# A graph layer on one core: slot numbers from smaller matmuls, edge rows evicted seven and six tiles at a time through two pairs of PSUM banks, loads on another queue

## The chip, the cores and the metric

The kernel runs on one core of a Trainium2 chip. The metric is the device time of one execution in microseconds (us). The kernel before takes 2601.75 us (median of 3 runs, 2600.41 to 2601.91). The profile shows one of these executions, the one of 2600.41 us.

A core has five engines that matter here: TensorE (PE in the profile, with PEld for its weight loads), VectorE (DVE), ScalarE (ACT), GpSimd (POOL) and SyncE (SP). ACT, SP and POOL also issue DMA transfers, each from a queue of its own.

## The reference

The reference is one graph layer with a residual and a layer norm. There are 6250 nodes with 64 features and 206250 directed edges (100000 both ways, and a loop at each node), sorted by destination, each with 64 edge features.

```
row, col = src, dst                       # per edge
msg  = concat(x[col], edge_attr)          # [206250, 128]
h    = relu(msg @ W1a.T + b1a) @ W1b.T + b1b
agg  = segment_sum(h, row) / max(count(row), 1)
z    = relu(concat(x, agg) @ W2a.T + b2a) @ W2b.T + b2b
out  = layernorm(x + concat(z, x) @ Wr.T + br)
```

The second matrix of the edge network is applied after the sum, so an edge contributes a row of 128 hidden values (after the ReLU) to the node `row`. The edges are sorted by `col`, so the rows have to be brought together by `row`.

## The kernel before

**Tiling.** The edges are cut into 1612 tiles of 128, and the tiles into 124 groups of 13. Nodes are numbered in 49 bins of 128. Since edges are sorted by destination, the destinations of one group lie in a window of few nodes: a group's right-hand operand `rhs` holds the 64 edge features of its 1664 edges and, below them, a one-hot row block that picks the node of the window; the weights `mv` hold W1a's edge half and the window's rows of x times W1a.

**The way of an edge row.** For each tile, one fp32 matmul (`hidden`, L949; the profile has two records for each) gives 128 edges by 128 hidden values in PSUM. ACT evicts several tiles at once with the ReLU into `orow` (L950). POOL then scatters the 13 tiles of a group into an array in device memory, one indirect DMA per tile (`scatter`, L956); an edge goes to a slot within the region of the bin of its source node. Later, SP reads the bins back (`read`, L1005), DVE makes a one-hot block from the node numbers (`nodes_of`, L1031 and L1034), TensorE sums the rows by node (`summed`, L1050), and DVE adds the partial sums (`collect`, L1106). Groups of such sums are called sum groups; an epoch is a run of groups that share a slot array (82, 17, 14, 7 and 4 groups).

**Slot numbers.** The slot of an edge is the number of edges with the same bin that come before it in its epoch. For group k, DVE writes a block of 50 bins by 14 columns: the first column of a bin carries the running count (L830), the other 13 say which tile's edge in this partition has this bin (`bins`, L831). A scan (L837) makes running sums from it (`had`). TensorE adds over partitions: with a matrix of ones on `had` (L850) and a matrix of "partition before" and a large diagonal on `bins` (L851), each in two halves of 25 bins, 350 and 325 columns, into two PSUM banks `cnt_ps`. The large diagonal lifts the entry of an edge's own bin above the rest, so one maximum over the bins (L867, in `slots`) picks it, and L872 turns it into the row number `rowidx` that the scatter uses.

**Order of the work.** PE, ACT, DVE and SP run in the order in which the program is written; POOL runs its scatters in order. One iteration k of the main loop does, in this order:

1. `group(k + 3)`: loads for three groups ahead. The edge features (`edges`, L700, 416 KB), the places in the window (L912, 208 KB), a register load (L916) and the window's table rows (L918). From group 8 on ACT issues them, before that SP.
2. ACT's cast of node numbers into `orow` (L1182).
3. TensorE's counting matmuls for group k + 1 (L850, L851).
4. `hidden` of group k in three parts of 4, 3 and 3 tiles.
5. `window(k + 2)` for the first groups, which have no table yet; DVE's `columns(k + 2)`, the one-hot block of `rhs` (L929), and `bins_of(k + 2)`.
6. For k = 6 to 18 a node step (`nodes_ahead`, L1150 to L1160): a matmul for x with W2a, one with Wr, and after DVE's negation a second matmul into the second half of the same PSUM tile.
7. The sum groups that are due, and after the first of them `slots(k + 1)`; after the second (or the first, if only one is due) the last part of `hidden`, 3 tiles, and then the 13 scatters.

After the loop come the remaining sums and the last node step for each three bins (means, transpose, two matrix layers, residual, layer norm, output).

**Buffers around the change.** PSUM: two banks for counting, two buffers for the sums, and the pool `hps` with three separate buffers of one bank each. Parts of `hidden`, windows, the node steps, the table rows (`y_rows`) and the tail all take their PSUM tiles from this pool in turn:

```
            for k0, n in parts:
                ps = hp.tile([P, SUB, H], F32, name="h_ps")
                ...
                nc.scalar.activation(orow[:, k0 : k0 + n, :H], ps[:, :n, :], AF.Relu)
```

SBUF: four `rhs` (EDGES), four `mv`, five `orow` (ROWS), nine read buffers (READS). A sum group is issued to SP when its reads fit in the READS buffers beside those that are still in use.

Of the kernel before, what the change touches and what calls it, by code (L numbers as in the profile page):

```python
# [8 lines left out]
F32 = mybir.dt.float32  # L9
# [8 lines left out]
P = 128  # L18
# [445 lines left out]
ROWS, EDGES, READS = 5, 4, 9  # L464
# [13 lines left out]
def fast_path(  # L478
# [161 lines left out]
    eye_b = const.tile([P, P], F32, name="eye_b")  # L640
    nc.vector.tensor_scalar(eye_b, diff_i, 0.0, BIG, op0=ALU.is_equal, op1=ALU.mult)
# [36 lines left out]
    with (  # L678
# [6 lines left out]
        tc.tile_pool(name="hps", bufs=3, space=PSUM) as hp,  # L685
# [11 lines left out]


        def edges(g):
            (nc.sync if g < NEAR else nc.scalar).dma_start(rhss[g % EDGES][:D, :], edgeT[:, g * NG * P : (g + 1) * NG * P])  # L700
# [25 lines left out]
        def y_rows(b_lo, b_hi):  # L726
            for b0 in range(b_lo, b_hi, SUB):
                n = min(SUB, b_hi - b0)
                ps = hp.tile([P, SUB, H], F32, name="h_ps")
# [26 lines left out]
        nc.vector.scalar_tensor_tensor(  # L756
            before_w, diff_i, 0.0, eye_b, op0=ALU.is_gt, op1=ALU.add
        )
        state = {"rt": 0, "bad": 3}
# [5 lines left out]
        none_b = const.tile([P, 2 * HALF], BF16, name="none_b")  # L765
        nc.vector.memset(none_b, 0.0)
# [52 lines left out]
        hads = {}  # L819

        def bins_of(k):


            ep_ = epoch_of[k]
            c0 = k * BLK
            oh = slp.tile([P, 2 * HALF * T], BF16, name="bins")
            had = slp.tile([P, 2 * HALF * T], BF16, name="had")
            by_bin = oh.rearrange("p (b t) -> p b t", t=T)
            was = none_b if k == ep_.first else state["had"][:, :, BLK]
            nc.vector.tensor_tensor(by_bin[:, :, 0], was, on.rearrange("p (b t) -> p b t", t=T)[:, :, 1], op=ALU.mult)  # L830
            nc.vector.tensor_tensor(  # L831
                by_bin[:, :, 1:],
                ramp[:, : 2 * HALF, None].to_broadcast([P, 2 * HALF, BLK]),
                hi[:, None, c0 : c0 + BLK].to_broadcast([P, 2 * HALF, BLK]),
                op=ALU.is_equal,
            )
            nc.vector.tensor_tensor_scan(had, on, oh, 0.0, op0=ALU.mult, op1=ALU.add)  # L837
            oh, had = (v.rearrange("p (b t) -> p b t", t=T) for v in (oh, had))
            state["had"] = hads[k] = had
            return oh, had  # L840

        def counts_of(oh, had):

            ps = slpp.tile([P, 2, 512], F32, name="cnt_ps")
            for i in range(2):
                v = ps[:, i, : HALF * T].rearrange("p (b t) -> p b t", t=T)
                b = slice(i * HALF, (i + 1) * HALF)
                nc.tensor.matmul(v, one_w, had[:, b, :], start=True, stop=False)  # L850
                nc.tensor.matmul(v[:, :, :BLK], before_w, oh[:, b, 1:], start=False, stop=True)  # L851
            return ps

        def slots(k, ps):
# [4 lines left out]
            if at == 0:  # L859
# [3 lines left out]
                    state["bin"], hi[:, c0 : c0 + m], float(STRIDE), -BIG, op0=ALU.mult, op1=ALU.add  # L863
                )
            v = ps[:, :, : HALF * T].rearrange("p i (b t) -> p i b t", t=T)
            row = slp.tile([P, T], F32, name="row")
            nc.vector.tensor_reduce(row, v.rearrange("p i b t -> p t i b"), axis=mybir.AxisListType.XY, op=ALU.max)  # L867

            def by_now(t):
                nc.vector.tensor_copy(t.rearrange("p (i b) -> p i b", i=2), v[:, :, :, BLK])  # L870

            s = nc.vector.scalar_tensor_tensor(  # L872
                rowidx[:, c0 : c0 + BLK], row[:, :BLK], BIG + STRIDE - 1,
                state["bin"][:, at : at + BLK], op0=ALU.min, op1=ALU.add,
            )
            state["slots"] = s.ins
            if k + 1 == EARLY:
                by_now(early)
                wrong(early, epochs[0].low, ALU.is_gt, slp)
            for st in ep_.steps[:-1]:  # L880
                if k + 1 == st.at:
                    full = slp1.tile([P, 2 * HALF], F32, name="full")
                    by_now(full)
                    wrong(full, st.hi, ALU.is_lt, slp)
            if k + 1 == ep_.end:
                by_now(ep_.tot)
                unused(ep_)

                if (ep_.end - ep_.first) * BLK > 255:
                    most = slp.tile([P, 2 * HALF], F32, name="most")  # L890
                    nc.vector.tensor_scalar(
                        most, hads[k][:, :, BLK], 255.5, None, op0=ALU.is_gt, op1=ALU.add,
                        accum_out=bad[:, state["bad"] :][:, :1],
                    )
                    state["bad"] += 1

        def group(g):
# [14 lines left out]
            s = nc.scalar.dma_start(  # L912
                rel, relt[g : g + 1, :].rearrange("o (h e) -> o h e", h=2).to_broadcast([WIN, 2, half])
            )
            with tc.issue_after(s.ins):
                w = nc.scalar.value_load(win_i[0:1, g : g + 1], min_val=0, max_val=N - WIN)  # L916
            m = mv[g % MV]
            nc.scalar.dma_start(m[D:, :], ytab[bass.ds(w, WIN), :])  # L918
# [15 lines left out]
        def window(g):  # L934

            ps = hp.tile([P, H], F32, name="h_ps")
# [239 lines left out]
        for k, ep_ in enumerate(epoch_of):  # L1176
# [11 lines left out]
            if k + 1 < NGR:  # L1188
                counts = counts_of(*ahead)
# [243 lines left out]
```

## Time and profile before

| | before |
|---|---|
| median of 3 runs | 2601.75 us |
| the profiled execution | 2600.41 us |
| its span, first to last instruction | 2598.5 us |
| mean granted TensorE clock | 0.713 |
| POOL: first scatter starts, last scatter ends | 17.5 us, 2477.7 us |
| POOL: one scatter, 1612 of them | 0.96 us |
| ACT: evictions L950 | 496, mean 0.516 us |
| DVE busy | 1174.2 us |
| bytes moved, mean rate | 375.22 MB, 144 GB/s |

The granted clock is the share of its full speed that TensorE was allowed; in the page's clock row each digit is one fortieth of the span, in tenths. A line of the group list names line, engine, operation, output and inputs, shapes and count; then busy time and the mean of one in ns; then the engine's idle time just before these instructions and what ended most of it. In the list of waits, the numbers are the total in us, how often, and the longest. "remote" is a releaser that the profile could not name. In the timeline the columns are start, duration, engine, line, operation, output and inputs, how many instructions the row joins, and in brackets the idle time before and what ended it.

### The profile page before, as it was taken

The numbers are of one execution on the slowest core, as the hardware profiler recorded it, in microseconds if no ns is written. First come the engines' busy times: TensorE is split into PE (matmuls) and PEld (weight loads), VectorE is DVE, ScalarE is ACT, GpSimd is POOL, SyncE is SP. The second block draws the span as 40 slices with busy tenths as digits, with TensorE's granted clock in tenths as the row PEclk, the third lists the DMA queues.
The fourth block names the chain that finished last, engine by engine and source line by source line (L and its number), as shares of the span: only waits on it lengthen the run. The fifth ranks groups of instructions, "written<-read, shape, count | busy, mean of one in ns | idle before, by whom it ended". The sixth has DMA issues, their size and how long they took to land.

```text
span 2598.5 us, 25106 instructions
## 1 busy us (share of the span) xinstructions
PE 1444.2 (56%) x8253; PEld 1265.4 (49%) x8253; DVE 1174.2 (45%) x1993; ACT 325.1 (13%) x807; POOL 1555.7 (60%) x1630
## 2 busy tenths in 40 slices
PE   3646553444455445454544566565566655666796
PEld 2535443334345344343444555564555555555795
DVE  5233343333334334343433444463545445545587
ACT  1211111111111010110110100110001000110106
POOL 6566666666666666666666665656556666666500
PEclk7656675666766667676766677786777777677898
DMA  6568556444444444343444455544545645555581
GB/s 160 158 207 259 167 164 186 139 115 124 115 121 134 118 117 121 108 133 107 135 125 115 128 157 148 155 136 118 141 143 144 176 139 142 151 151 152 170 261 39
DMA packets 198784, 375.22 MB, mean 144 GB/s; under 512 B 47098, under 2 KB 113980, under 8 KB 198516
## 3 DMA queue, kind: packets, MB, share of 16 engines
q1 hardware_dynamic: 86050, 145.73, 20.1%
q10 hardware_dynamic: 61010, 120.39, 17.2%
q0 software_dynamic: 51584, 107.40, 13.1%
q8 instruction: 67, 1.10, 0.2%
q14 instruction: 73, 0.60, 0.1%
HBM read 221.77 MB, written 151.59 MB: 144 GB/s over the span
## 4 chain that ended last, share of the span: by engine, by line
PE 30%; another core or an unknown queue 28%; issue 18%; DVE 14%; DMA 3%; ACT 3%; ACTq 2%; SPq 0%; DVEq 0%
PE sum_ps L1050 13%; PE h_ps L949 12%; DVE oh L1034 4%; DVE rhs L929 3%; DMA rhs<-relt 2%; DVE had L837 2%; ACT orow L950 2%; PE cnt_ps L851 1%; PE cnt_ps L850 1%; DVE part L1106 1%; DVE row L867 1%; DVE bins L831 1%; PE h_ps L1159 1%; DMA rt<-rows 1%
## 5 line engine op out<-in xcount | busy, mean ns | idle before, releaser
L956 POOL DMA_INDIRECT rows<-orow,rowidx x1612 | 1547.8, 960 | 921.4 <-issue 452.3
L949 PE MATMUL h_ps<-mv,rhs 128*128 128x128 f32 x3224 | 639.8, 349 | 612.7 <-issue 400.2
L949 PEld LDWEIGHTS h_ps<-mv,rhs 128*128 128x128 f32 x3224 | 573.7, 257 | 689.2 <-issue 458.9
L1050 PE MATMUL sum_ps<-rt,oh 128*128 128x129 f32 x4006 | 615.3, 309 | 265.8 <-issue 233.7
L1050 PEld LDWEIGHTS sum_ps<-rt,oh 128*128 128x128 f32 x4006 | 574.1, 223 | 294.1 <-issue 256.8
L950 ACT ACTIVATE orow<-h_ps 128x512 f32<-128x512 f32 x496 | 239.5, 516 | 1814.5 <-remote 1025.1
L1106 DVE TENSOR_TENSOR part<-part,sum_ps 128x258 f32<-128x258 f32 (+2 forms) x183 | 86.4, 473 | 512.0 <-remote 352.8
L929 DVE TENSOR_TENSOR rhs<-rhs,ramp 64x1664 f32<-64x1664 bf16 x116 | 219.4, 1892 | 186.8 <-DMA rhs<-relt 113.2
L867 DVE TENSOR_REDUCE row<-cnt_ps 128x14 f32<-128x700 f32 x124 | 109.3, 882 | 344.7 <-remote 272.2
L837 DVE TENSOR_TENSOR_SCAN had<-ramp,bins 128x700 bf16<-128x700 bf16 x124 | 200.3, 1615 | 4.2
L1034 DVE TENSOR_TENSOR oh<-ramp,node 128x512 f32<-128x512 f32 (+3 forms) x237 | 187.3, 790 | 8.0
L1034 DVE TENSOR_TENSOR oh<-ramp,rt 128x512 f32<-128x512 f32 (+3 forms) x213 | 137.1, 693 | 4.7 <-issue 4.6
L850 PE MATMUL cnt_ps<-had,one_w 128*128 128x350 bf16 x248 | 96.8, 393 | 68.4 <-issue 49.1
L851 PE MATMUL cnt_ps<-bins,before_w 128*128 128x325 bf16 x248 | 97.8, 397 | 39.0 <-issue 38.1
L831 DVE TENSOR_TENSOR bins<-ramp,hi 128x650 bf16<-128x650 f32 x124 | 108.2, 873 | 0.0
L1031 DVE SCALAR_TENSOR_TENSOR node<-unused,rt 128x4 f32<-128x4 bf16 (+3 forms) x237 | 37.4, 158 | 136.5 <-DMA rt<-rows 126.3
L851 PEld LDWEIGHTS <-before_w 128*128 128x128 bf16 x248 | 28.4, 115 | 90.0 <-issue 78.6
L1155 DVE TENSOR_SCALAR zT<-h_ps 128x512 f32<-128x512 f32 (+1 forms) x13 | 8.6, 661 | 123.3 <-PE h_ps L1154 72.4
L1182 ACT CAST orow<-lo 128x13 f32<-128x13 bf16 x124 | 26.6, 214 | 301.8 <-issue 136.8
L1150 PE MATMUL h_ps<-zT,w2x_t 65*128 65x512 f32 (+1 forms) x26 | 21.8, 936 | 73.2 <-ACT orow L950 68.7
L850 PEld LDWEIGHTS <-one_w 128*128 128x128 bf16 x248 | 29.7, 120 | 65.8 <-issue 56.9
L830 DVE TENSOR_TENSOR bins<-had,ramp 128x50 bf16<-128x50 bf16 x119 | 44.1, 371 | 3.6
(113 smaller groups left out, 393.9 us busy)
## 6 DMA issues: line engine op xcount, KB each, us to landing
rt<-rows SPq DMA_DIRECT2D x242, 260.0 KB
rhs<-in_edgeT ACTq DMA_DIRECT2D x116, 416.0 KB
rt<-rows SPq DMA_DIRECT2D x106, 390.0 KB
rows<-orow,rowidx POOLq DMA_INDIRECT x1612
rhs<-relt ACTq DMA_DIRECT2D x116, 208.0 KB
rows<-padrow ACTq DMA_DIRECT2D x4, 4680.0 KB
rows<-padrow ACTq DMA_DIRECT2D x8, 2340.0 KB
rt<-rows SPq DMA_DIRECT2D x48, 325.0 KB
```

The lines of the kernel that those rows point to most:

```text
L831: nc.vector.tensor_tensor(by_bin[:, :, 1:], ramp[:, : 2 * HALF, None].to_broadcast([P, 2 * HALF, BLK]), hi[:, None, c0 : c0 + BLK].to_broa ...
L837: nc.vector.tensor_tensor_scan(had, on, oh, 0.0, op0=ALU.mult, op1=ALU.add)
L850: nc.tensor.matmul(v, one_w, had[:, b, :], start=True, stop=False)
L851: nc.tensor.matmul(v[:, :, :BLK], before_w, oh[:, b, 1:], start=False, stop=True)
L867: nc.vector.tensor_reduce(row, v.rearrange("p i b t -> p t i b"), axis=mybir.AxisListType.XY, op=ALU.max)
L929: nc.vector.tensor_tensor(rhs[D:, :].rearrange("p (h e) -> p h e", h=2), rel, in_win[D:, :, None].to_broadcast([WIN, 2, NG * P // 2]), op= ...
L949: nc.tensor.matmul(ps[:, j, :], rhs[:, c * P : (c + 1) * P], m, start=True, stop=True)
L950: nc.scalar.activation(orow[:, k0 : k0 + n, :H], ps[:, :n, :], AF.Relu)
L956: s = nc.gpsimd.indirect_dma_start(out=ep_.rows, out_offset=bass.IndirectOffsetOnAxis(ap=rowidx[:, t : t + 1], axis=0), in_=orow[:, j, :], ...
L1034: nc.vector.tensor_tensor(res[:, at_tile : at_tile + nb * n, :], ramp[:, None, :].to_broadcast([P, nb * n, P]), node[:, :, None].to_broadc ...
L1050: nc.tensor.matmul(of_bin(b), oh[:, at_tile, :], rt[:, j * n + t, : H + 1], start=t0 + t == st.lo[b], stop=t0 + t == st.hi[b] - 1,)
L1106: nc.vector.tensor_add(to, to, g.ps[:, : g.nb, :])
```

## The change

**Slots.** The scan now starts from zero in every group, so it gives an edge's number within its partition and bin (`nth`). A running total of 50 bins per partition is kept in a small tile `had` (one operation of 50 columns per group). The count of edges before those of this partition, the base, comes from two matmuls of 50 columns into one PSUM tile: ones on the totals of the groups before, and "partition before" on this group's counts. DVE then adds base and number for 13 edges by 50 bins, lifts the entry of an edge's own bin with a multiply-add, and takes the maximum. The totals over all partitions, which some checks at 11 places need, get a matmul of their own there (`counted`). The tiles of the 13 columns are two persistent ones, set to zero once.

**Edge rows.** The pool `hps` has one tile of four banks. `bank(n)` hands out the next n banks of it in turn. A group's `hidden` has two parts, of 7 and 6 tiles, each in two banks and evicted by one ACT operation; the part of 6 comes where the last part of 3 was. Everything else that used the pool takes one bank, and a node step takes three.

**Loads.** SP issues all of a group's loads, in front of the reads of iteration k. There are 8 read buffers instead of 9.

```
-ROWS, EDGES, READS = 5, 4, 9
+ROWS, EDGES, READS = 5, 4, 8
...
-        tc.tile_pool(name="hps", bufs=3, space=PSUM) as hp,
+        tc.tile_pool(name="hps", bufs=1, space=PSUM) as hp,
...
+        banks = hp.tile([P, 4, 512], F32, name="h_ps")
+        state = {"rt": 0, "bad": 3, "bank": 0}
+
+        def bank(n=1):
+            i = -(-state["bank"] // n) * n % 4
+            state["bank"] = (i + n) % 4
+            return banks[:, i : i + n, :].rearrange("p i f -> p (i f)")
...
-            (nc.sync if g < NEAR else nc.scalar).dma_start(rhss[g % EDGES][:D, :], ...)
+            nc.sync.dma_start(rhss[g % EDGES][:D, :], ...)
...
         def bins_of(k):
-            nc.vector.tensor_tensor(by_bin[:, :, 0], was, on..., op=ALU.mult)
             nc.vector.tensor_tensor(
-                by_bin[:, :, 1:],
+                ohs[k % 2][:, :, 1:],
...
-            nc.vector.tensor_tensor_scan(had, on, oh, 0.0, op0=ALU.mult, op1=ALU.add)
+            nc.vector.tensor_tensor_scan(
+                nth, on, ohs[k % 2].rearrange("p b t -> p (b t)"), 0.0, op0=ALU.mult, op1=ALU.add
+            )
...
+                nc.vector.scalar_tensor_tensor(
+                    had, hads[k - 1], 1.0, nths[k][:, :, BLK], op0=ALU.mult, op1=ALU.add
+                )
...
-                nc.tensor.matmul(v, one_w, had[:, b, :], start=True, stop=False)
-                nc.tensor.matmul(v[:, :, :BLK], before_w, oh[:, b, 1:], start=False, stop=True)
+        def bases_of(k):
+            if k > 0:
+                counted(k - 1)
+            first_ = k == epoch_of[k].first
+            if not first_:
+                nc.tensor.matmul(bases, one_w, hads[k - 1], start=True, stop=False)
+            nc.tensor.matmul(bases, before_w, nths[k][:, :, BLK], start=first_, stop=True)
...
-            nc.vector.tensor_reduce(row, v.rearrange("p i b t -> p t i b"), axis=mybir.AxisListType.XY, op=ALU.max)
+            nc.vector.tensor_tensor(
+                own, bases[:, :, None].to_broadcast([P, 2 * HALF, BLK]), nths[k][:, :, 1:], op=ALU.add
+            )
+            nc.vector.scalar_tensor_tensor(own, ohs[k % 2][:, :, 1:], BIG, own, op0=ALU.mult, op1=ALU.add)
+            row = slp.tile([P, BLK], F32, name="row")
+            nc.vector.tensor_reduce(row, own.rearrange("p b t -> p t b"), axis=mybir.AxisListType.X, op=ALU.max)
...
         def group(g):
-            s = nc.scalar.dma_start(
+            s = nc.sync.dma_start(
...
-            nc.scalar.dma_start(m[D:, :], ytab[bass.ds(w, WIN), :])
+            nc.sync.dma_start(m[D:, :], ytab[bass.ds(w, WIN), :])
...
         def hidden(k, parts):
-                ps = hp.tile([P, SUB, H], F32, name="h_ps")
+                ps = bank(2).rearrange("p (j h) -> p j h", h=H)
...
         def nodes_ahead(b0):
-            xp = hp.tile([P, 2, SUB, D], F32, name="h_ps")
+            xp, np_ = (bank().rearrange("p (j d) -> p j d", d=D) for _ in range(2))
...
-                hidden(k, ((0, 4), (4, 3), (7, 3)))
+                hidden(k, ((0, 7),))
...
-                        hidden(k, ((10, 3),))
+                        hidden(k, ((7, 6),))
```

## The prediction

> **What bounds the kernel now.** I read the page first: busy shares, clock row, costliest groups.
>
> ```profile
> PE 1444.2 (56%) x8253; PEld 1265.4 (49%) x8253; DVE 1174.2 (45%) x1993; ACT 325.1 (13%) x807; POOL 1555.7 (60%) x1630
> ...
> PEclk7656675666766667676766677786777777677898
> ...
> L956 POOL DMA_INDIRECT rows<-orow,rowidx x1612 | 1547.8, 960 | 921.4 <-issue 452.3
> L950 ACT ACTIVATE orow<-h_ps 128x512 f32<-128x512 f32 x496 | 239.5, 516 | 1814.5 <-remote 1025.1
> L867 DVE TENSOR_REDUCE row<-cnt_ps 128x14 f32<-128x700 f32 x124 | 109.3, 882 | 344.7 <-remote 272.2
> L837 DVE TENSOR_TENSOR_SCAN had<-ramp,bins 128x700 bf16<-128x700 bf16 x124 | 200.3, 1615 | 4.2
> L831 DVE TENSOR_TENSOR bins<-ramp,hi 128x650 bf16<-128x650 f32 x124 | 108.2, 873 | 0.0
> L830 DVE TENSOR_TENSOR bins<-had,ramp 128x50 bf16<-128x50 bf16 x119 | 44.1, 371 | 3.6
> ```
>
> No engine is full. POOL issues 1612 scatters of 0.96 us with 0.30 us between them: 1.266 us each, 16.46 us per group of 13, 2041 us in all. Its first starts at 17.5 us, its last ends at 2477.7; what remains is a tail of 121 us. Its other idle time is 422 us in 119 stalls, and the list of waits names the cause:
>
> ```profile
> ACT orow L950 <- remote: 1025.1, 104, 24.7
> ACT orow L950 <- PE h_ps L949: 548.9, 85, 17.5
> ...
> POOL rows L956 <- ACT orow L950: 405.1, 120, 14.4
> ...
> PEld h_ps L949 <- ACT orow L950: 220.3, 30, 16.6
> PE h_ps L949 <- ACT orow L950: 208.3, 28, 16.3
> ```
>
> POOL waits for ACT's evictions, ACT for TensorE. Of the stalls, 76 stand before a group's tile 10 (the part that is computed behind the sums) and 36 before tile 0. The timeline of one cycle shows their form:
>
> ```profile
> 1042.18 0.95 POOL L956 DMA_INDIRECT rows<-orow,rowidx  x1 [0.30 <-issue]
> ...
> 1045.75 0.49 ACT L950 ACTIVATE orow<-h_ps 128x384 f32<-128x384 f32 x1 [15.21 <-remote]
> ...
> 1046.52 0.95 POOL L956 DMA_INDIRECT rows<-orow,rowidx  x1 [3.38 <-ACT orow L950]
> ...
> 1048.66 1.35 ACT L950 ACTIVATE orow<-h_ps 128x512 f32<-128x512 f32 x3
> ...
> 1069.73 1.36 ACT L950 ACTIVATE orow<-h_ps 128x512 f32<-128x512 f32 x3 [6.46 <-remote]
> 1070.61 0.96 POOL L956 DMA_INDIRECT rows<-orow,rowidx  x1 [4.21 <-ACT orow L950]
> ```
>
> POOL runs dry at 1043.13; ACT and DVE's L867 get TensorE's results only 2.62 us later, both at 1045.75, and POOL restarts at 1046.52. The second stall is alike: dry at 1066.40, results at 1069.73. Between stalls TensorE runs at its own pace for about 5 us after POOL's restart and then crawls: from about 1079 to 1101 its matmul records come 0.7, 1.4 or 2.1 us apart, and at 1101.66, after POOL ran dry at 1099.33, 17 retire in one row of 4.76 us. So while POOL issues scatters, TensorE's completions hardly come through. A stall of 3.4 to 5 us releases them, and how many tiles POOL may then scatter depends on how much hidden-layer work TensorE finished, or had already done unseen. At 1048.66 three evictions of the next group follow at once: that run-ahead exists because three separate PSUM tiles take the parts. From group 26 to 73 three stalls come per four groups, gaps 3.4, 4.2 and 4.9 us, bursts of 16, 23 and 13 tiles (19.3 us per group). From group 76 on a stall comes at tile 10 of nearly every group, gaps mostly 3.6 us, some 5.3 (20.5 us per group).
>
> **The change part by part.**
>
> *PSUM.* The diff makes four banks one tile, and a pair of banks takes a part. In the instruction list of the changed program the first matmul of group 55's first part (upper pair) waits for the eviction of group 54's second part (lower pair), and the second part for the eviction of the first: each part waits for the part just before, not for the one before that. In the old program a part waits for the part three back. So no part can be computed unseen behind one that is not yet evicted. Behind the waiting matmul stand, in TensorE's order, the sums, the other part and the next group's counting; ACT, DVE and POOL wait for those. The eviction itself grows: 0.49 us for 384 columns and 0.59 for 512 give by their slope about 0.79 for 768 and 0.89 for 896, so +0.3 us in each stall.
>
> Groups 19 to 76 (58): after a restart with the second part (6 tiles, 7.6 us), TensorE has to do the next first part (14 records: 20 took 2.39 us at 1073.97 and 3.20 at 1866.79, so 1.7 to 2.2), its eviction (0.89), 24 sum records (3.58 at 1047.74), and the second part (12 records, some 1.7). That is about 8 us against the 5 us of open pace: the first part gets through, the second does not, and POOL stalls once per 13 tiles at tile 7. With gaps between the 3.6 us of the late groups and the mean of 4.2 here, 3.9 less the ordinary 0.3, plus 0.3: 16.46 + 3.9 = 20.36, against 19.3 now: +1.06 x 58 = **+61**. Ends: bursts as now with +0.3 in 44 stalls, +13; two stalls per group (16.46 + 7.8 = 24.3), +290.
>
> Groups 77 to 123 (47) stall once per group already: +0.3 x 47 = +14. If every other 3.6 us gap becomes the 5.3 of its neighbours, +40 more. I take **+25**, nearer to the rows as they are.
>
> The 13 early node steps (k = 6 to 18) lose their own tiles: the second matmul batch now waits for DVE's read of the first (0.66 us, L1155), and the third for ACT's copy: one more round trip each. It costs 0.7 us in the open stretch, up to the 5.6 us between two evictions at 419.50 and 425.15 in the crawl. I take 2: **+26**. Windows, the y rows and the tail: the tail's chain (transpose, copy, matmul, max, matmul, add) already runs in that order, 4.00 us per step, bound by DVE: **+5** (0 to +20).
>
> *Counting.* Four matmuls of 350 and 325 columns (0.31 us each at full clock, 0.50 at half) become two of 50, plus 11 totals. This saves about 0.6 us of TensorE in the open stretch, or two crawling pairs of 1.4 us. POOL gains only where that lets a part through; ends 0 and 0.6 x 124 = -75. I take a third: **-25**.
>
> DVE loses L830 (0.371) for a running total of the same 50 columns, about equal, and gains an addition and a multiply-add of 650 elements in place of nothing (nearest row L831, 0.873: +1.75 us); the reduce stays near 0.88. That is near +1.8 us per group in an engine that is 45% busy. Its cover: row numbers are wanted only when POOL reaches the next group's tile 0, now 6 tiles (7.6 us) after a restart, against 3 tiles before. **0**; if DVE's order delays the sums behind it, up to 1.8 x 124 = +223. Several of these operations read two SBUF inputs while POOL works. Row: the scan L837, which also has two, ran from 1053.84 to 1055.45, and the scatters at 1054.08 and 1055.34 kept 0.96 us and gaps of 0.30.
>
> A rule that speaks against the change: the Trainium skill, "SBUF — State Buffer", section "Who interferes with whom", has a DVE instruction with two SBUF inputs contend with a GpSimd instruction that reads SBUF, one blocking the other whole. If the new multiply-add blocked POOL for its 0.87 us, estimated from that page's rule, the sum would rise by about 108 us; the row above shows no such block, and the sum goes by the row.
>
> *Loads and reads.* ACT loses three issues (0.48, 0.62 and 0.49 us and a register load: 2.3 us between 1045.78 and the next cast at 1048.55). That stood before the next part's eviction. POOL's 36 stalls at tile 0 could each gain it (-83), but the next part is now not computed by then: **-10** (end 0). On SP the loads stand in front of the iteration's reads and wait for the previous group's second part; the reads behind them need them gone. With 8 read buffers, groups of three reads have two in flight rather than three. The waits of today are small (relt 113.2 us in 30 waits, rt 126.3 in 31), so **+10**, from 0 to +126 if the second doubles.
>
> Sum: 61 + 25 + 26 + 5 - 25 + 0 - 10 + 10 = +92, on the profiled execution's own 2600.41 (span 2598.5): 2692. The median of the runs is 1.3 us higher.
>
> **The rivals.**
>
> *Longer bursts (faster).* TensorE has fewer columns to stream, and a released part is 6 or 7 tiles rather than 3 or 4. If groups 19 to 76 reach 20 tiles per burst rather than 17, they lose 6 stalls (-24); if the late ones reach 17 rather than 13, 11 of 47 (-40). With -35 from counting and ACT, +28 for eviction and +26 for the node steps: 2555. For it: 23-tile bursts exist. Against it: they come from run-ahead. It decides if a part, its eviction, the sums and the next part fit in the 5 us.
>
> *Two stalls per group.* Both parts miss the open stretch: +290 in the middle, and 47 x 3.6 = +169 late: about 3060. Against: 20 records fitted at 1073.97.
>
> *DVE or SP late.* The sums wait for DVE's longer order or late loads: half of +223 on top of half the +92: 2760. For: L929 waits for relt already. Against: DVE is idle 55%.
>
> *Nothing moves.* The compiled wait is there, but parts were rarely ahead, and savings pay for eviction: 2603.
>
> **How the numbers follow.** The forecast gets 0.50, longer bursts 0.20, DVE or SP late 0.16, two stalls 0.09, nothing moves 0.05. The likeliest one's own range is 2640 to 2745. Leaving out two stalls and a slice of each end, the range is 2555 to 2810. Within 0.2%, about what a measurement of this kernel can tell from no change: 0.05; faster 0.20; slower 0.75.
>
> **What the profile after would show.** Right: POOL's stalls at tile 7 of nearly every group, gaps of 3.6 to 4.5 us, waits of the hidden layer's matmuls for ACT above today's 208, ACT evictions 248 of 0.8 to 0.9 us, scatters still 0.96. Wrong: bursts over 17 tiles in the middle, or stalls ended by DVE's row numbers, or the open stretch reaching much beyond 5 us because completions come through otherwise.

## The result and the profile after

The changed kernel takes 2677.23 us (median of 4 runs, 2673.34 to 2685.33) against 2601.08 us for the kernel before in the same comparison: a ratio of 1.0305, with a 95% interval of 1.0272 to 1.0338. (Here and below the ratios are estimates from all runs of a comparison, so they differ slightly from the quotient of the two medians.) By the medians it is slower by 76 us. The forecast was slower, with 2692 us and a range of 2555 to 2810.

The profiled execution took 2685.33 us, with a span of 2683.5. Its page, with the same groups as before:

```profile
PE 1377.8 (51%) x8011; PEld 1265.4 (47%) x8011; DVE 1449.1 (54%) x2241; ACT 295.6 (11%) x559; POOL 1581.3 (59%) x1630
...
PEclk7566556567676666766676777777677777777965
...
L970 POOL DMA_INDIRECT rows<-orow,rowidx x1612 | 1573.4, 976 | 918.5 <-issue 463.3
...
L964 ACT ACTIVATE orow<-h_ps 128x896 f32<-128x896 f32 x248 | 214.5, 865 | 2128.8 <-remote 1479.8
...
L840 DVE TENSOR_TENSOR_SCAN nth<-ramp,bins 128x700 bf16<-128x700 bf16 x124 | 200.3, 1616 | 4.3
...
L905 DVE TENSOR_REDUCE row<-own 128x13 f32<-128x650 f32 x124 | 158.2, 1276 | 4.3
...
L903 DVE SCALAR_TENSOR_TENSOR own<-bins,own 128x650 f32<-128x650 bf16 x124 | 103.8, 837 | 4.3
```

A reader should see three things. The evictions are 248 of 0.865 us, near the forecast. The scatters (L970) have become longer: 0.976 us in the mean instead of 0.960, 25.6 us over all 1612; the forecast had them stay at 0.96. And the clock row, which ended in 898 before, ends in 965.

The list of waits after:

```profile
ACT orow L964 <- remote: 1479.8, 110, 22.5
PEld h_ps L963 <- ACT orow L964: 779.6, 109, 19.7
PE h_ps L963 <- ACT orow L964: 728.0, 107, 19.4
...
POOL rows L970 <- ACT orow L1197: 272.4, 73, 6.5
...
POOL rows L970 <- ACT orow L964: 120.2, 24, 26.5
```

The wait that was predicted is there: the hidden layer's matmuls now wait 728 us for ACT instead of 208. POOL stalls at tile 7 of a group in 90 cases, where the forecast had nearly every one of the 124 groups, and at tile 0 in 25, which it did not have. But POOL's stalls together (116 of them, 417.6 us) are no longer than before (119, 421.8 us). So the wait is real, and it is not what costs the time. The time, divided at the scatters of the trace (in the loop, the stretches are groups; us):

| stretch | before | after | difference | of it longer scatters |
|---|---|---|---|---|
| start to the first scatter | 17.5 | 18.9 | +1.4 | |
| groups 0 to 5 | 124.6 | 140.7 | +16.1 | +1.3 |
| groups 6 to 18 | 250.0 | 257.8 | +7.8 | +1.7 |
| groups 19 to 76 | 1121.9 | 1129.5 | +7.6 | +9.8 |
| groups 77 to 123 | 963.8 | 953.5 | -10.3 | +12.8 |
| after the last scatter | 120.8 | 183.1 | +62.3 | |

Three quarters of the loss lie in the tail, to which the prediction gave 5 us. The tail in both kernels, by the timeline; first before, a bit over one step of 4.00 us:

```profile
2542.59 0.52 DVE L1302 TENSOR_TENSOR zT<-zT,h_ps 128x384 f32<-128x384 f32 x1
...
2543.03 0.35 DVE L1310 TENSOR_TENSOR y<-h_ps,xr 128x192 f32<-128x192 f32 x1
...
2543.75 0.49 PE L1295 MATMUL h_ps<-ident,agg 128*128 128x128 f32 x3
...
2544.16 0.30 PEld L1301 LDWEIGHTS h_ps<-aT,wam_t 128*128 128x128 f32 x2 [0.16 <-ACT aT L1297]
2544.16 0.91 PE L1301 MATMUL h_ps<-aT,wam_t 128*128 128x384 f32 x2
...
2544.91 0.78 PE L1308 MATMUL h_ps<-wzz_t,zT 128*128 128x64 f32 x6
...
2546.58 0.53 DVE L1302 TENSOR_TENSOR zT<-zT,h_ps 128x384 f32<-128x384 f32 x1
```

and after, a bit over one step of 8.67 us (most of the steps there take 7.6 to 8.7 us):

```profile
2585.65 0.85 PE L1312 MATMUL h_ps<-ident,agg 128*128 128x128 f32 x3
...
2587.50 0.46 ACT L1314 COPY aT<-h_ps 128x384 f32<-128x384 f32 x1
...
2588.01 1.65 PE L1318 MATMUL h_ps<-aT,wam_t 128*128 128x384 f32 x2 [1.51 <-ACT aT L1314]
2589.70 0.56 DVE L1319 TENSOR_TENSOR zT<-zT,h_ps 128x384 f32<-128x384 f32 x1 [3.19 <-PE h_ps L1318]
2590.30 1.35 PEld L1325 LDWEIGHTS h_ps<-wzz_t,zT 128*128 128x128 f32 x6 [1.80 <-DVE zT L1319]
2590.30 1.54 PE L1325 MATMUL h_ps<-wzz_t,zT 128*128 128x64 f32 x6 [0.65 <-DVE zT L1319]
...
2591.88 0.36 DVE L1327 TENSOR_TENSOR y<-h_ps,xr 128x192 f32<-128x192 f32 x1 [1.63 <-PE h_ps L1325]
...
2594.32 0.85 PE L1312 MATMUL h_ps<-ident,agg 128*128 128x128 f32 x3
```

Before, TensorE does a transpose, a layer and a residual in one go of 1.9 us, with no wait in brackets at any of the matmuls (one weight load waits 0.16 us): they belong to three different groups of bins, each a stage further. After, the layer waits for ACT's read of the transposes (1.51 us) and the residual for DVE's read of the layer (0.65 us). Each time that is another group's work, and the wait is there because all three now use one tile. And TensorE, idle in between, is granted less clock: mean 0.71 over the stretch after the last scatter, against 0.95 before; the six records of a residual take 1.54 us instead of 0.78. The windows of that stretch, before and after; the columns are its length, the busy time of PE, PEld, DVE, ACT and POOL with counts, granted clock, DMA share and GB/s:

```profile
2477.70:2598.50 120.80, 96.43 (x728) 86.24 (x726) 98.17 (x348) 44.73 (x133) 0.04 (x1) 0.95 0.48 149
```

```profile
2500.50:2683.50 183.00, 131.37 (x701) 110.60 (x701) 96.89 (x341) 44.71 (x133) 0.00 (x0) 0.71 0.32 95
```

**Chips.** The runs below did not all fall on a chip like the first one. On two others the kernel before takes 2147 to 2154 us instead of 2580 to 2601, and in the profiles taken there (of changed kernels; the nearest to the kernel before is the one with the loads moved) POOL's long stalls are missing: scatters follow each other at 0.30 us almost from first to last, and TensorE's results are not held back. So each kernel is compared only with the kernel before on its own chip, and it is said whether that chip is one with stalls.

### The profile page after: what moved, and what is told of

Read it like the earlier page. It is cut to its first block, busy times and chain, and to the rows that moved or that the text cites. A ratio compares the mean times of both kernels' runs of the same rounds, so it can differ in the third digit from the quotient of the medians.

```text
span 2683.5 us, 24187 instructions
## 1 busy us (share of the span) xinstructions
PE 1377.8 (51%) x8011; PEld 1265.4 (47%) x8011; DVE 1449.1 (54%) x2241; ACT 295.6 (11%) x559; POOL 1581.3 (59%) x1630
## 4 chain that ended last, share of the span: by engine, by line
another core or an unknown queue 49%; PE 17%; issue 13%; DVE 10%; ACT 6%; POOL 2%; DMA 1%; ACTq 0%; SPq 0%; DVEq 0%; POOLq 0%
PE h_ps L963 9%; PE sum_ps L1064 5%; ACT orow L964 4%; DVE oh L1048 3%; POOL rows L970 2%; DVE rhs L943 1%; DVE nth L840 1%; PE h_ps L1325 1%; DVE part L1120 1%; PE h_ps L1318 1%; DMA rt<-rows 1%; PE h_ps L739 1%; DVE row L905 1%; DMA rows<-orow,rowidx 1%
## 5 line engine op out<-in xcount | busy, mean ns | idle before, releaser
L970 POOL DMA_INDIRECT rows<-orow,rowidx x1612 | 1573.4, 976 | 918.5 <-issue 463.3
L1064 PE MATMUL sum_ps<-rt,oh 128*128 128x129 f32 x4006 | 583.0, 308 | 105.0 <-issue 90.8
L964 ACT ACTIVATE orow<-h_ps 128x896 f32<-128x896 f32 x248 | 214.5, 865 | 2128.8 <-remote 1479.8
L1048 DVE TENSOR_TENSOR oh<-ramp,rt 128x512 f32<-128x512 f32 (+3 forms) x213 | 147.4, 706 | 293.4 <-DMA rt<-rows 208.4
L848 DVE SCALAR_TENSOR_TENSOR had<-had,nth 128x50 bf16<-128x50 bf16 x119 | 29.6, 249 | 372.3 <-remote 268.9
L840 DVE TENSOR_TENSOR_SCAN nth<-ramp,bins 128x700 bf16<-128x700 bf16 x124 | 200.3, 1616 | 4.3
L1048 DVE TENSOR_TENSOR oh<-ramp,node 128x512 f32<-128x512 f32 (+3 forms) x237 | 187.4, 791 | 7.8
L905 DVE TENSOR_REDUCE row<-own 128x13 f32<-128x650 f32 x124 | 158.2, 1276 | 4.3
L900 DVE TENSOR_TENSOR own<-cnt_ps,nth 128x650 f32<-128x650 f32 x124 | 102.6, 828 | 6.9 <-remote 6.9
L903 DVE SCALAR_TENSOR_TENSOR own<-bins,own 128x650 f32<-128x650 bf16 x124 | 103.8, 837 | 4.3
L1045 DVE SCALAR_TENSOR_TENSOR node<-unused,rt 128x4 f32<-128x4 bf16 (+3 forms) x237 | 38.7, 163 | 123.5 <-DMA rt<-rows 92.6
L833 DVE TENSOR_TENSOR bins<-ramp,hi 128x650 bf16<-128x650 f32 x124 | 103.5, 834 | 2.1
L885 PE MATMUL cnt_ps<-had,one_w 128*128 128x50 bf16 x119 | 24.7, 208 | 91.3 <-DVE own L900 34.7
L886 PE MATMUL cnt_ps<-nth,before_w 128*128 128x50 bf16 x124 | 31.0, 250 | 36.8 <-DVE at L782 22.1
```

The costliest lines, as they stand in the source:

```text
L833: nc.vector.tensor_tensor(ohs[k % 2][:, :, 1:], ramp[:, : 2 * HALF, None].to_broadcast([P, 2 * HALF, BLK]), hi[:, None, c0 : c0 + BLK].to_ ...
L840: nc.vector.tensor_tensor_scan(nth, on, ohs[k % 2].rearrange("p b t -> p (b t)"), 0.0, op0=ALU.mult, op1=ALU.add)
L900: nc.vector.tensor_tensor(own, bases[:, :, None].to_broadcast([P, 2 * HALF, BLK]), nths[k][:, :, 1:], op=ALU.add)
L903: nc.vector.scalar_tensor_tensor(own, ohs[k % 2][:, :, 1:], BIG, own, op0=ALU.mult, op1=ALU.add)
L905: nc.vector.tensor_reduce(row, own.rearrange("p b t -> p t b"), axis=mybir.AxisListType.X, op=ALU.max)
L970: s = nc.gpsimd.indirect_dma_start(out=ep_.rows, out_offset=bass.IndirectOffsetOnAxis(ap=rowidx[:, t : t + 1], axis=0), in_=orow[:, j, :], ...
```

## The experiments

**Separate tiles in the tail.** Two comparisons, both on a chip without stalls; the second has the changed kernel as well.

```
-        tc.tile_pool(name="hps", bufs=1, space=PSUM) as hp,
...
+        hp = by_slot.enter_context(tc.tile_pool(name="hps", bufs=1, space=PSUM))
...
         by_slot.close()
+        with tc.tile_pool(name="nw", bufs=3) as nw, tc.tile_pool(name="tps", bufs=3, space=PSUM) as tp:
...
-                    tr = bank()[:, : SUMS * P]
+                    tr = tp.tile([P, SUMS * P], F32, name="h_ps")
...
```

(p1, p3 and the last sum in the same way.)

> The changed kernel, but the node steps after the loop take three separate one-bank PSUM tiles in turn instead of banks of the one shared tile. Theory (the shared tile puts the three stages of a node step, which belong to three different groups of bins, in a single chain): the steps after the last scatter go back from 8 us to about 4.0 us each, the stretch after the last scatter from 183 to about 121 us, the time to 2677 - 62 = 2615. Rival (the tail is long since the sums come late there, with 8 read buffers or DVE's longer order, and the clock falls from that): the steps stay at 7 to 8 us, and the time within 10 us of 2677.

> The changed kernel with three separate one-bank tiles in the tail, beside the changed kernel on the same chip. Theory: 60 to 65 us faster than it on either kind of chip; on a chip with stalls some 10 to 25 us slower than the kernel before, most of it from the first ten groups.

> The changed kernel once more, so that it stands beside the others on one chip: the earlier runs with changed PSUM tiles fell on a chip on which the kernel before takes 2147 us instead of 2601, its scatters never stall, and TensorE's results are not held back. Theory, on a chip with stalls: 1.03 times the kernel before, 62 us of it after the last scatter. On a chip without stalls: the tail's 62 to 65 us, and 19 to 25 us of longer scatters, which then have nothing to hide in: about 85 us over the kernel before, 2232. The prediction's view (the loop's stall pattern) would give no loss in the loop on a chip without stalls.

The changed kernel takes 2235.74 us there against 2154.49: a ratio of 1.0379 (1.0362 to 1.0397), +81 us, where 2232 was expected. With separate tiles in the tail it is 2173.93, 1.0095 (1.0078 to 1.0112); in the first comparison 2167.73 against 2146.83, 1.0097 (1.0080 to 1.0114). The edit gives back 62 us. Windows of the stretch after the last scatter, the changed kernel and then the one with separate tiles:

```profile
2083.00:2228.00 145.00, 90.49 (x379) 70.60 (x379) 62.25 (x258) 44.70 (x133) 0.00 (x0) 0.64 0.20 58
```

```profile
2082.00:2166.00 84.00, 58.35 (x379) 49.31 (x379) 60.81 (x258) 44.69 (x133) 0.00 (x0) 0.87 0.35 100
```

The same 379 matmul records and 258 DVE instructions take 145 us in one tile and 84 in three, with the clock at 0.64 and 0.87. The rival (the sums come late) falls: loads, reads and DVE's order are the same in both.

**Two tiles for the pairs in the loop as well.**

```
-        banks = hp.tile([P, 4, 512], F32, name="h_ps")
+        banks = [hp.tile([P, 2, 512], F32, name=f"h_ps{i}") for i in range(2)]
...
-            i = -(-state["bank"] // n) * n % 4
-            state["bank"] = (i + n) % 4
-            return banks[:, i : i + n, :].rearrange("p i f -> p (i f)")
+            state["bank"] += 1
+            return banks[state["bank"] % 2][:, :n, :].rearrange("p i f -> p (i f)")
```

> As the run with separate tiles in the tail, and in the loop the two pairs of banks are two tiles, taken in turn, so that a part of the hidden layer waits for the part two back and not for the one just before. The prediction's step (the shared tile costs about 1 us for each group from 19 to 76, and 26 us in the early node steps) says that the loop gets shorter by 60 to 100 us: about 2530. The theory after seeing the profile (most of the loop's loss is longer scatters; the shared tile costs something in the first ten groups, where the table rows are made one bank at a time) says 10 to 30 us: about 2590 to 2605, with waits of the hidden layer's matmuls for ACT falling to under 300 us from 728.

> The same with two separate pair tiles in the loop. On a chip without stalls the same time as with the tail alone (2167 for both, already seen). On a chip with stalls the prediction's step says 60 to 100 us faster than with the tail alone, the theory 10 to 30, mostly in the first ten groups.

2167.32 us in the first comparison and 2174.37 in the second (1.0095 of the kernel before in both): the same as with the tail alone. On a chip without stalls the loop is bound by POOL's scatters and does not feel the shared tile at all. Both runs fell on such a chip, so the expected 10 to 30 us on a chip with stalls were not put to the test.

**The shared tile alone.** The kernel before, with its three banks as one tile:

```
-        tc.tile_pool(name="hps", bufs=3, space=PSUM) as hp,
+        tc.tile_pool(name="hps", bufs=1, space=PSUM) as hp,
...
+        banks = hp.tile([P, 3, 512], F32, name="h_ps")
+        ring = {"at": 0}
+        def bank():
+            ring["at"] += 1
+            return banks[:, ring["at"] % 3, :]
...
-                ps = hp.tile([P, SUB, H], F32, name="h_ps")
+                ps = bank().rearrange("p (j h) -> p j h", h=H)
...
```

> The kernel before, with its three one-bank buffers made into one tile of three banks that are handed out in turn: the shared tile alone, with parts of 4, 3, 3 and 3 tiles, the old counting and the old loads. Theory: the tail grows by the same 50 to 65 us, as node steps of 8 us, the first ten groups by 10 to 20; and the loop pays too, since four parts per group wait one behind the other: 20 to 100 more. In all 2680 to 2780. Rival (the shared tile does not matter, the parts of 7 and 6 and the queue order do): within 15 us of 2601.

> The kernel before with its three banks as one tile. On a chip without stalls +73, already seen: 65 in the tail and 7 in the loop. On a chip with stalls: the same 65 in the tail; the loop by the prediction's step at least 60 more (four parts, each waiting for the one before), by the theory under 30.

2219.56 us against 2146.83, 1.0345 (1.0328 to 1.0362), and again 2219.17 against 2154.49, 1.0301 (1.0284 to 1.0318). The stretch after the last scatter is 151.2 and 149.3 us, against 86.1 in the run with the loads moved, which is as fast as the kernel before on that chip. So one tile in place of three, with nothing else of the change, costs the tail its 64 us. The guess of 20 to 100 us in the loop was wrong for this chip: the last scatter ends at 2065 us instead of 2058. What one tile costs the loop on a chip with stalls was not measured.

**The loads on SP's queue**, in the kernel before: the three `dma_start` of `group` and its register load go from `nc.scalar` to `nc.sync`.

> The kernel before, with all loads of a group on SP's queue in front of the reads, and nothing else. The prediction gave the loads' move -10 on ACT and some of +10 on SP: within 15 us of 2601. If ACT's issues (2.3 us before the next part's eviction) were on the path: up to -80. If the loads hold back the reads: DVE's waits for read rows grow from 126 us, and the time with them by up to 60 us.

2146.37 us against 2146.83: 0.9997 (0.9988 to 1.0007), on a chip without stalls. Moving the loads is worth nothing there. Its list of waits shows what the hidden layer waits for when nothing holds TensorE's results:

```profile
ACT orow L1182 <- DMA rows<-orow,rowidx: 1454.5, 113, 15.2
PEld h_ps L949 <- ACT orow L950: 731.9, 106, 12.4
PE h_ps L949 <- ACT orow L950: 711.7, 105, 12.2
```

ACT waits for the scatters to leave one of the five `orow` tiles, and TensorE waits for ACT: all of it is ahead of POOL. Here TensorE waits as long for ACT as in the changed kernel with stalls (728 us), at no cost. A long wait in the list is not yet a loss. The same holds for DVE's waits for read rows, which the expectation feared: they are 671.9 us here (L1031 and L1034), against 147.8 in the first run of the shared tile alone, which leaves the loads on ACT, and the time is that of the kernel before.

**Eight read buffers**, in the kernel before:

```
-ROWS, EDGES, READS = 5, 4, 9
+ROWS, EDGES, READS = 5, 4, 8
```

> The kernel before with 8 read buffers instead of 9, nothing else. Groups of three reads have two in flight instead of three. Expected small: 0 to +15 us on 2601. If reads in flight hide device memory latency that nothing else hides, DVE's waits for read rows (126 us in 31 waits) double, and the time grows by 30 us or more.

2578.03 us against 2579.64 on a chip with stalls: 0.9999 (0.9971 to 1.0027). If there is a difference, it is under 8 us. DVE's waits for read rows are 358.2 us in this profile (126.3 in the kernel before, on the first chip); here, too, they more than doubled without the 30 us that were expected of that.

**A DVE operation with two inputs in SBUF, and one with a single input there.** On top of the eight read buffers, in the kernel before, ahead of the maximum L867:

```
+        extra = slp1.tile([P, 2 * HALF, BLK], F32, name="extra")
+        nc.vector.memset(extra, 0.0)
...
+            nc.vector.scalar_tensor_tensor(extra, ohs[k][:, :, 1:], 1.0, extra, op0=ALU.mult, op1=ALU.add)
```

and in the second kernel the last input is `ramp[:, : 2 * HALF, None].to_broadcast([P, 2 * HALF, BLK])`, which lies in PSUM.

> The kernel before with 8 read buffers, and one more DVE operation for each group, whose result nothing uses: a multiply-add of 650 elements with both inputs in SBUF (the block of bins in bf16, a scratch tile in fp32, written in place). Theory (a DVE operation with two SBUF inputs and POOL's scatter hold each other up): some 70 or more scatters take 1.2 to 1.6 us instead of 0.96, as in the changed kernel, the mean scatter rises by 0.010 to 0.020 us, and the time by 15 to 30 us over the run with 8 read buffers alone. Rival (it is only 0.84 us more of DVE work for each group): scatters stay at 0.96 and the time within 8 us of that run. The Trainium skill, page SBUF - State Buffer, section Who interferes with whom, states the theory's rule.

> As the run with the unused multiply-add, but its second input is read from PSUM (the number ramp, broadcast), so that one input is in SBUF. Same elements, same place in DVE's order. Theory: no scatter is longer than in the kernel before beyond its first groups (10 over 1.05 us), and the time is within 8 us of the run with 8 read buffers. Rival (DVE's time itself costs): the same time as with two SBUF inputs.

On the scatters the theory holds. With two inputs in SBUF, 63 scatters take over 1.05 us, with one 10, and with the eight buffers alone 12. The groups of both kernels, two inputs first:

```profile
L960 POOL DMA_INDIRECT rows<-orow,rowidx x1612 | 1569.5, 974 | 878.7 <-issue 462.3
...
L869 DVE SCALAR_TENSOR_TENSOR extra<-bins,extra 128x650 f32<-128x650 bf16 x124 | 102.8, 829 | 0.0
```

```profile
L960 POOL DMA_INDIRECT rows<-orow,rowidx x1612 | 1553.0, 963 | 895.9 <-issue 455.3
...
L869 DVE SCALAR_TENSOR_TENSOR extra<-bins,ramp 128x650 f32<-128x650 bf16 x124 | 102.1, 823 | 0.0
```

The operation itself takes the same time in both (0.829 and 0.823 us). On the time the theory fails on this chip, which is one with stalls: 2572.89 us with two inputs, 0.9962 (0.9934 to 0.9990) of the kernel before, and 2588.77 with one, 1.0037 (1.0012 to 1.0062); against the eight buffers alone that is -5 us, where +15 to +30 was expected, and +11, where at most 8 was. The kernel with 16.5 us more scatter time is the faster one. In its profile POOL's stalls are shorter by as much (378.7 us instead of 396.0), though the execution profiled is the slowest of its ten. That a lengthened scatter falls into time that a stall would have taken is a reading that fits, not one that was shown.

**Slot numbers without two SBUF inputs.** The changed kernel with separate tiles in the tail and for the pairs, and the sums `own` made in two halves of 25 bins in the free part of the counting bank:

```
-        counts = slpp.tile([P, 2, 2 * HALF], F32, name="cnt_ps")
+        counts = slpp.tile([P, 512], F32, name="cnt_ps")
+        own = counts[:, 4 * HALF :][:, : HALF * BLK].rearrange("p (b t) -> p b t", t=BLK)
...
+            for i in range(2):
+                b = slice(i * HALF, (i + 1) * HALF)
+                nc.vector.tensor_tensor(
+                    own, bases[:, b, None].to_broadcast([P, HALF, BLK]), nths[k][:, b, 1:], op=ALU.add
+                )
+                nc.vector.scalar_tensor_tensor(own, ohs[k % 2][:, b, 1:], BIG, own, op0=ALU.mult, op1=ALU.add)
+                nc.vector.tensor_reduce(rows[:, i, :], own.rearrange("p b t -> p t b"), axis=mybir.AxisListType.X, op=ALU.max)
...
```

> The changed kernel with separate tiles in the tail and two pair tiles in the loop, and the slot numbers made in two halves of 25 bins in the free part of the counting bank, so that neither the addition nor the multiply-add has two inputs in SBUF. Theory (two SBUF inputs lengthen the scatters): fewer than 15 scatters over 1.05 us, mean 0.960 us. On a chip without stalls the time falls by the 19 to 25 us of the longer scatters, to within 6 us of the kernel before. Rival (the longer order of DVE, not its inputs, costs there): 15 to 25 us slower than the kernel before, as without this edit. On a chip with stalls the prediction's step (the shared tile costs the loop 60 us or more) would make this kernel 10 to 40 us slower than the kernel before at most, or faster; the theory says within 15 us of it.

2152.22 us against 2153.38, on a chip without stalls: 0.9995 (0.9986 to 1.0004). Eleven scatters take over 1.05 us, instead of 69 and 75 in the two runs with pair tiles, and the last one ends at 2065.4 us instead of 2079.5 and 2087.1. (Those two were on the other chip of that kind; the mean scatter is 0.964 us here, 0.960 was expected.) DVE has eight operations for a group's slots there instead of four, so it was not DVE's own time that cost. On such a chip longer scatters are paid in full, as far as a comparison across two chips can tell. With this the whole change, its PSUM tiles and operands put right, is as fast as the kernel before and not faster; no version of the change beat it.

## Why the prediction was right, point by point

The direction, and by size the total, came out (+92 predicted, +76 measured by the medians, +85 between the profiled executions). The sum did not: two errors cancel in it, and that the total is so near is luck. The mechanism, parts that wait for one another because they share a tile, was right; where it costs time was not.

- *What bounds the kernel.* POOL's stalls behind held-back results were read rightly for this chip, but that other chips do not have them could not be seen in one trace.
- *The shared tile.* The step "each part waits for the part just before" was right, in the loop and in the program's waits; the price in the loop was mis-sized. Groups 19 to 76: predicted +61, measured +7.6, and 9.8 us of longer scatters are in that, so the stalls cost nothing more than before. The forecast's 58 stalls of 3.9 us beyond the ordinary gap would be 226 us; the trace has 49 with 168.0 us in all, and before 46 with 170.1. The step "about 8 us against the 5 us of open pace" failed in part of the cycles. After the stall before 1224.65 us, TensorE did the first part, the sums and the second part at its own pace, until 1232.9:

```profile
1223.56 0.81 ACT L964 ACTIVATE orow<-h_ps 128x768 f32<-128x768 f32 x1 [20.46 <-remote]
...
1224.43 3.35 PE L963 MATMUL h_ps<-mv,rhs 128*128 128x128 f32 x14 [13.53 <-ACT orow L964]
1224.65 0.96 POOL L970 DMA_INDIRECT rows<-orow,rowidx  x1 [4.83 <-ACT orow L1197]
...
1227.57 3.96 PE L1064 MATMUL sum_ps<-rt,oh 128*128 128x129 f32 x24
1227.88 0.92 ACT L964 ACTIVATE orow<-h_ps 128x896 f32<-128x896 f32 x1 [3.40 <-issue]
...
1231.37 1.50 PE L963 MATMUL h_ps<-mv,rhs 128*128 128x128 f32 x12
...
1238.95 0.81 ACT L964 ACTIVATE orow<-h_ps 128x768 f32<-128x768 f32 x1 [10.16 <-remote]
```

  The open stretch was at least 8 us here, and the second part's eviction came while POOL was still at work, 6 us later. So from group 26 to 73 bursts of 19 and 20 tiles stand among those of 13: 15 of 43 bursts. That is the point from which the rival "longer bursts" was said to decide, and it was met about every third time. In the mean the bursts still got shorter, 14.5 tiles against 16.8 in 37 bursts before; the gaps before them shrank too, from 4.05 to 3.58 us.
- *Groups 77 to 123*: predicted +25, measured -10.3, with 12.8 us of longer scatters in it. The stalls there fell from 192.8 to 169.8 us. Whether fewer counting columns or ACT's missing loads did it was not taken apart.
- *Node steps in groups 6 to 18*: predicted +26, measured +7.8.
- *Windows, table rows, tail*: predicted +5, measured +62.3 in the tail and +16.1 in groups 0 to 5. This is the step that failed outright. "The tail's chain already runs in that order" is true of one group of bins and overlooked that the three stages in one round belong to three groups; the shared tile makes them a chain. The early groups seem to pay in the same coin: the table rows' copies, 1.71 us apart before, as at 96.34 and 98.05 us, come every 2.75 us after, and POOL's stall before group 4 grows from 14.4 to 26.5 us. That the one makes the other is not shown: on a chip without stalls the changed kernel's copies are 2.75 us apart as well, and its groups 0 to 5 take 104.5 us, against 103.5 with the loads moved.

```profile
96.34 0.59 ACT L735 COPY part<-h_ps 128x512 f32<-128x512 f32 x1 [1.12 <-PE h_ps L732]
98.05 0.59 ACT L735 COPY part<-h_ps 128x512 f32<-128x512 f32 x1 [1.12 <-PE h_ps L732]
```

```profile
95.31 0.59 ACT L742 COPY part<-h_ps 128x512 f32<-128x512 f32 x1 [2.16 <-PE h_ps L739]
...
98.06 0.59 ACT L742 COPY part<-h_ps 128x512 f32<-128x512 f32 x1 [2.17 <-PE h_ps L739]
```

- *DVE*: the cover held: the list of POOL's waits puts 392.6 us to ACT and 51.3 to DVE (before, 41.5 to DVE). DVE's work was sized too low: it is busy 2.2 us more per group instead of 1.8, mostly since the maximum takes 1.276 us and not the 0.88 that it kept in the forecast. The argument against the rule was wrong. The prediction took the scan as a row with two inputs in SBUF; its second input, `on`, is a view of the tile `steady`, which the kernel keeps in PSUM (the group list names that tile "ramp"). None of the long DVE operations of the kernel before has two inputs in SBUF, so the row said nothing. The new multiply-add has two. The Trainium skill (page "SBUF — State Buffer", section "Who interferes with whom") has such an operation contend with a GpSimd instruction that reads SBUF. This case's runs show it: 81 scatters over 1.05 us instead of 10, and 25.6 us more of scatter time. That is far under the 108 us of the forecast's estimate, in which every operation blocks for its whole length. The trace says why: 88 scatters were already running when a multiply-add began, and none of them got longer; 85 started inside one, 76 of these were lengthened, by 0.33 us each in the mean.

```profile
1233.18 0.84 DVE L903 SCALAR_TENSOR_TENSOR own<-bins,own 128x650 f32<-128x650 bf16 x1
...
1233.48 1.37 POOL L970 DMA_INDIRECT rows<-orow,rowidx  x1 [0.31 <-DMA rows<-orow,rowidx]
```

  Here a scatter that started inside the multiply-add took 1.37 us.
- *The other rivals.* Two stalls per group did not come (116 stalls in 124 groups), and DVE's wait for the loads (`relt`) fell from 113.2 to 6.6 us. But its waits for the reads, which now stand behind the loads on SP's queue, grew from 126.3 (L1031) to 301.0 us (L1045 and L1048). That is the doubling for which the prediction held up to +126 us ready, and it did not cost that: of POOL's waits 25.0 us are put to the two lines. The lists, before and after:

```profile
DVE node L1031 <- DMA rt<-rows: 126.3, 31, 27.2
...
DVE rhs L929 <- DMA rhs<-relt: 113.2, 30, 8.2
```

```profile
DVE oh L1048 <- DMA rt<-rows: 208.4, 65, 7.5
...
DVE node L1045 <- DMA rt<-rows: 92.6, 44, 5.9
```

  "Nothing moves" is what happened in the loop from group 19 on: -2.7 us.
- *Counting, loads, reads* (-25, -10, +10): the loads' move and the eighth read buffer measured nothing, each by itself, the first on a chip without stalls and the second on one with. Counting was not measured alone.

Left open: why TensorE's results are held back on some chips, and whether that stays with a chip; what lengthens the early groups; and what the shared tile costs the loop on a chip with stalls once the tail is mended, since all runs with separate tiles fell on chips without stalls.

## What to carry to other kernels

Where stages of different items run in one round, count the buffers by item and not by stage: one tile split by index is one buffer to the waits, even where the banks differ. Before a row of the trace is used against a rule, look up in the code in which memory each operand lies; a name in the profile does not say it. And check a sum by stretches, not by its total: here +61 that did not come and +62 that was not seen gave the right answer.

## What the runs showed of the hardware

- The same kernel takes 2580 to 2601 us where its scatters stall and 2147 to 2154 on two other chips. The scatters take 0.960 us on both kinds; what differs is POOL's stalls (422 us in the kernel before, against 1 us in the profile with moved loads) and the tail, 121 against 86 us in the same two.
- A DVE operation of 650 elements with both inputs in SBUF (L903, 0.84 us) lengthens the scatters that start inside it: 76 of 85 took over 1.0 us, 1.29 in the mean, and the earlier the start, the longer; the time from the operation's start to the scatter's, with the extra time added, comes to about 0.71 us. Of the 88 scatters already running none got longer, and the operation was not held either (0.836 to 0.879 us). With one input in PSUM (L869 of the second kernel with the extra operation) none of the 81 scatters that started inside it got longer.
- TensorE's granted clock is lower where its stages wait for each other in the tail: 0.71 against 0.95 when three stages run in one go (without stalls 0.64 against 0.87); the same records then take up to twice as long (1.54 against 0.78 us).
- The maximum over 650 elements in SBUF takes 1.276 us (L905), that over 700 in PSUM 0.882 (L867). The two also differ in layout, so it is not shown that the memory makes the difference.
